# Four attention layers over a 4096-node graph on one core: first products before x, second layer's outputs through PSUM, third layer's rows through DRAM, last masks loaded earlier

## The chip, the core and the metric

The kernel runs on one core of a Trainium2 chip. TensorE (PE) multiplies, VectorE (DVE), ScalarE (ACT) and GpSimd (POOL) work on tiles in on-chip memory (SBUF, and PSUM, into which PE writes), and SyncE (SP) starts most of the transfers from DRAM. Each engine works through its own list of instructions in order and waits for others by semaphores. The metric is the device time of one execution in microseconds (us), lower is better: 2969.83 before, the median of three runs from 2969.72 to 2972.38.

## What is computed

`x` is 4096x256, `adj` a symmetric 4096x4096 matrix of 0 and 1 with ones on the diagonal. Each of four layers attends over the graph's neighbours, adds its input and normalises each row:

```python
def gat(h, adj, W, a):                     # layer 1: 4 heads
    Wh = (h @ W).reshape(n, heads, d)
    e = leaky_relu(s_i[:, None, :] + s_j[None, :, :], 0.2)   # s_i, s_j: Wh times the halves of a
    alpha = softmax(where(adj == 0, -inf, e), axis=1)
    return elu(einsum('ijh,jhd->ihd', alpha, Wh))
def multi_head(x, edge, Wq, bq, Wk, bk, Wv, bv):             # layer 2: 4 heads of 64
    scores = einsum('hnd,hmd->hnm', q, k) / sqrt(64) + (edge.T - 1) * 10000
    return softmax(scores) @ v
# layer 3: as layer 1 with one head of 256 and slope 0.01
def cosine(f, adj, Wq, Wk):                # layer 4
    att = softmax(where(adj > 0, norm(f @ Wk.T) @ norm(f @ Wq.T).T, -9e15))
    return 0.5 * att @ f + 0.5 * f
for layer in (gat, multi_head, gat_one, cosine):
    x = layernorm(x + layer(x))
```

All products are in fp32.

## The kernel before

The rows of the state lie in the SBUF tile `X`, 32 tiles of 128 rows, with one more column of a constant that gives the sums of weights in the last layer. Each layer works on eight blocks `b` of 512 query nodes (`QW`), and in each block on units `j`: 32 tiles of 128 key nodes, in the second layer 64 tiles of 64. A unit builds the unnormalised weights of its keys for the block's queries (`weights`) and then multiplies them with the keys' values into sums in PSUM (`sums`), some units later. At the end of a block its sums are taken out of PSUM, and dividing, adding and normalising them (`outputs`, `finish`) happen in steps between the units of the next block. The outputs of a layer's last block are made in a `tail`, which the next layer calls at a place of its choice.

**First layer** (`additive_heads`, 0 to 727 us). Nodes have two exponentials, `src` and `dst`; a weight is formed from `row`, the `src` values of the block's queries laid along a row and repeated over all partitions (L248), and multiplied with the mask on DVE (L249). For `b` >= 1 the rows go through DRAM (`rows`, L229). For the first block `first_rows` makes them with transposes of broadcast columns (L226), copied out of PSUM at L227. The start runs: L317, one product that spreads the row of `a` over the partitions; `attach` (L101), which multiplies it into the weights on DVE; `turn(0)`, eight transposes of `X` (L111) and their copies to `xT` (L112); `prepare(0)`, eight products of 128x128 by 264 columns (L169, in four groups of key tiles, contraction halves `c` inside); `first_rows`. PE's order is fixed by hand here and in the second layer, elsewhere a scheduler puts the engines' work in order from the program. `narrow` (L816) makes POOL copy one column of a finished weight tile (`tick`) and lets a transfer follow it: the second layer's masks, narrowed to bytes in DRAM.

**Second layer** (`multi_head_attention`; its loop from 822 to 1748 us). A unit is eight matmuls for the scores (L561), the exponential in PSUM on ACT (L563), the mask product on DVE (L566, from PSUM to `prob` in SBUF) and, three units later, eight matmuls for the sums (L587). The sums of the weights, `den`, are gathered beside this: every even unit by POOL (L573, an addition of two SBUF tiles), every odd one by a transfer that accumulates (L579, which POOL issues). The score tiles `p` rotate through three PSUM buffers of two banks each. `finish` takes one of these buffers for the block before, through `halves()`: at j=12 for the sums of `den` (L603), at j=14 for their transposes and reciprocals (L611, L613), at j=17 and 19 for the transposes of half of the block's outputs (L619) each, which DVE multiplies with the reciprocals into the SBUF tile `oh` (L622) and adds to `X` (L627). The roots of the normalising begin at j=29 and end at j=33 (`end_root`, L129 to L132). DVE's and ACT's order is fixed by hand as well.

**Third layer** (`additive_one`, to 2276 us). `prepare(b)` makes `xT`, the values and the rows of one block, four row transposes at L382 among them. Two blocks are prepared first, then comes the second layer's `tail` (L603, L611, L619 and the normalising) and the start of the fourth layer (`follow.start`: its pools and two weight loads on SP), then the loop; during the first block's units the other six blocks are prepared. A unit is four matmuls of 257 columns (L400). A mask transfer on SP covers four units, 1 MB. The sums lie in four banks of the pool `pa` for even blocks and in the four banks `g` of `ps` for odd ones. In the last block, `follow.prepare` makes the fourth layer's inputs for six blocks, at every fifth unit, in the banks of `pa`.

**Fourth layer** (`cosine_attention`). `Cosine.prepare` makes `xT`, queries and keys (L719), their norms (`inverse_root`: L129 to L132) and their transposes `T` (L734). A unit is a product for the scores (L758), an exponential on ACT (L761), the mask on DVE (L762) and, two units later, four matmuls into the sums (L769). A mask transfer, issued by POOL, covers eight units. The third layer's `tail` (the last block's `add_elu` and normalising, small operations of DVE and ACT) and the preparation of the last two blocks come after the second and the thirteenth unit of the first block.

Of the kernel before, what the change touches and what calls it, by code (L numbers as in the profile page):

```python
# [9 lines left out]
FP = mybir.dt.float32  # L10
# [18 lines left out]
def kernel(  # L29
# [53 lines left out]
    def load_x(b, n=QB):  # L83
        for k in range(b * QB, (b + 1) * QB, n):
            nc.sync.dma_start(X[:, k:k + n, :D], xv[:, k:k + n, :])

    def load_w(sb, w, eng):
        eng.dma_start(sb, w.rearrange("(c p) f -> p c f", p=P))
# [73 lines left out]
    def additive_values(xT, b, groups, w_sb, V, src, dst, H, slope):  # L162

        g = 1.0 - slope
        heads = "p k (h d) -> p k h d"
        for k, n, pw in groups:
            for i in range(n):
                for c in range(KC):
                    nc.tensor.matmul(pw[:, i, :D + 2 * H], xT[:, c, (k + i) * P:(k + i + 1) * P], w_sb[:, c, :],  # L169
                                     start=(c == 0), stop=(c == KC - 1))  # L170
# [18 lines left out]
    def additive_heads(a, H, slope, early, narrow, ahead):  # L189
# [7 lines left out]
        with ExitStack() as lay:  # L197
# [23 lines left out]
            def first_rows():  # L221
                row[0] = rp.tile([P, H, QW], FP, name="row")
                for h in range(H):
                    pr = side[:, h, :] if h < HC + 1 else bank()
                    for k in range(QB):
                        nc.tensor.transpose(pr[:, k * P:(k + 1) * P], src[:, k, h:h + 1].to_broadcast([P, P]), ident)  # L226
                    (nc.scalar.copy if h % 2 else nc.vector.tensor_copy)(row[0][:, h, :], pr)  # L227
# [86 lines left out]
            with tc.manual_schedule(engines={mybir.EngineType.PE}):  # L314

                side = pa.tile([P, HC + 1, QW], FP, name="acc")
                nc.tensor.matmul(side[:, 0, :], ones[:1, :], a_row, start=True, stop=True)  # L317
                attach(keep, w_sb, side[:, 0, :], H)
# [4 lines left out]
                for i in range(len(units) + LAG):  # L323
                    if i < len(units):
                        b, j = units[i]
                        weights(b, j)
                        if (b, j) == (1, 4 * QB):
                            early()
                        if i % 8 == 4:
                            narrow(prob[b, j])  # L330
                    if i >= LAG:
# [22 lines left out]
    def additive_one(w_sb, slope, tail, op, follow):  # L354

        MJ = 4
        mvs, taken = {}, {}
        with ExitStack() as lay:
# [6 lines left out]
            sb = pool(lay, "gb_sb", 2)  # L365
            mp = pool(lay, "gb_mask", 3)

            pa = pool(lay, "gb_pa", 1, space=PSUM)
            ps = pool(lay, "gb_ps", 4, space=PSUM)
            edges = adjT.rearrange("(t p) i -> p t i", p=P)  # L370
# [5 lines left out]
            def prepare(b):  # L376
                xT = transposed_block(sb, bank, b)
                groups = [(k, 1, bank().rearrange("p (n f) -> p n f", n=1)) for k in range(QB)]
                additive_values(xT, b, groups, w_sb, V, src, dst, 1, slope)
                pr = bank()  # L380
                for k in range(QB):
                    nc.tensor.transpose(pr[:, k * P:(k + 1) * P], src[:, b * QB + k, :].to_broadcast([P, P]), ident)  # L382
                nc.scalar.copy(row[:, b * QW:(b + 1) * QW], pr)

# [37 lines left out]
            prepare(1)  # L422
            tail(bank)
            follow.start()
            turn = itertools.count()
            units = [(b, j) for b in range(NB) for j in range(NT)]
            for i in range(len(units) + 1):
                if i < len(units):
                    b, j = units[i]
                    weights(b, j)  # L430
                    if b == 0 and j % QB == 2 and j // QB + 2 < NB:
                        prepare(j // QB + 2)
                if i:
                    b, j = units[i - 1]
                    sums(b, j)
                    if b and j % 4 == 0 and j // 4 < QB:
                        outputs(b - 1, j // 4)

                    if b == NB - 1 and j % 5 == 3:
                        follow.prepare(even_bank, j // 5)  # L440
                    if j == NT - 1:
                        take_all(b)
# [7 lines left out]
    def multi_head_attention(w_sb, b_sb, tail, rows_of_den, narrow_edges):  # L450
# [12 lines left out]
        with ExitStack() as lay:  # L463
# [142 lines left out]

            def reciprocals(bank, b):
                s = kept[b]
                pd = bank()
                for k in range(QB):  # L610
                    nc.tensor.transpose(pd[:, k * P:(k + 1) * P], s[:, KC, k * P:(k + 1) * P], ident)  # L611
                rden[b] = fin.tile([P, QB, H], FP, name="rden4")
                nc.vector.reciprocal(rden[b].rearrange("p k h -> p (k h)"), pd[:, ::G])  # L613

            def half(bank, b, k):
                po = bank().rearrange("p (k f) -> p k f", f=D)
                for i in range(2):
                    for c in range(KC):
                        nc.tensor.transpose(po[:, i, c * P:(c + 1) * P],  # L619
                                            kept[b][:, c, (k + i) * P:(k + i + 1) * P], ident)  # L620
                o = fin1.tile([P, 2, D], FP, name="oh")
                nc.vector.tensor_tensor(o.rearrange("p k (h d) -> p (k h) d", h=H),  # L622
                                        po.rearrange("p k (h d) -> p (k h) d", h=H),
                                        rden[b][:, k:k + 2, :].rearrange("p k h -> p (k h)").unsqueeze(2)
                                        .to_broadcast([P, 2 * H, d]), OP.mult)
                y = X[:, b * QB + k:b * QB + k + 2, :D]
                nc.vector.tensor_tensor(y, y, o, OP.add)  # L627

# [6 lines left out]
            def finish(b, j):  # L635
# [4 lines left out]
                elif j == 12:  # L640
                    row_sums(halves(), b)
                elif j == 14:
                    reciprocals(halves(), b)
                elif j in (17, 19):
                    half(halves(), b, j - 17)
                elif j in (21, 23, 25, 27):
# [32 lines left out]
        def tail(bank):  # L679
# [3 lines left out]
            row_sums(bank, b)  # L683
            reciprocals(bank, b)
            half(bank, b, 0)
            half(bank, b, 2)
            mv = fin.tile([P, QB, 2], FP, name="mv")
# [6 lines left out]
    class Cosine:  # L694


        def __init__(self, stack):
            self.stack = stack

        def start(self):  # L700
            keep = self.stack.enter_context(tc.tile_pool(name="co_keep", bufs=1, side="right", reuse_waits="tile"))
            self.pool = self.stack.enter_context(tc.tile_pool(name="co_in", bufs=2, side="right", reuse_waits="tile"))
            self.T = keep.tile([P, 2, N], FP, name="T")
            self.w_sb = keep.tile([P, KC, 2 * P], FP, name="w3_sb")
            load_w(self.w_sb[:, :, :P], wq3T, nc.sync)
            load_w(self.w_sb[:, :, P:], wk3T, nc.sync)

        def prepare(self, bank, b):
# [28 lines left out]
    def cosine_attention(co, tail):  # L737
        MJ = 8
        T, in_ = co.T, co.pool
        with ExitStack() as lay:  # L740
# [3 lines left out]
            pa = pool(lay, "co_pa", 1, space=PSUM)  # L744
            edges = adjT.rearrange("(t p) i -> p t i", p=P)
            ov = out.rearrange("(t p) d -> p t d", p=P)
            mask, acc, prob, y = {}, {}, {}, {}

# [3 lines left out]
            def weights(b, j):  # L752
                cols = slice(b * QW, (b + 1) * QW)
                if j % MJ == 0:
                    mask[b, j // MJ] = sb.tile([P, MJ, QW], BF, name="mask")
                    nc.gpsimd.dma_start(mask[b, j // MJ], edges[:, j:j + MJ, cols])  # L756
                p = bank() if b and j % 2 else pz.tile([P, QW], FP, name="p")
# [3 lines left out]
                nc.scalar.activation(z, p, AF.Exp)  # L761
                nc.vector.tensor_tensor(z, z, mask[b, j // MJ][:, j % MJ, :], OP.mult)  # L762

# [49 lines left out]

    tick = const.tile([P, 1], FP, name="tick")

    def narrow(z):  # L816

        seen = nc.gpsimd.tensor_copy(tick, z[:, 0, :1])  # L818
        for b, j in itertools.islice(todo, 1):
            slim_edges[b, j] = slim.tile([P // 2, NJ, QW], U8, name=f"edges{b}_{j}")  # L820
            with tc.issue_after(getattr(seen, "ins", seen)):
                nc.gpsimd.dma_start(slim_edges[b, j],
# [78 lines left out]
```

## Time and profile before

| | |
|---|---|
| median of the runs | 2969.83 us (2969.72 to 2972.38, three runs) |
| the profiled execution | 2971.39 us |
| its span in the trace | 2969.5 us |
| loops of the layers in the trace | first to 727, second 822 to 1748, third 1748 to 2276, fourth from 2276 |
| a unit of the second layer's loop on PE | 16 matmuls, L561 591 ns and L587 589 ns each by the records, which overlap |
| POOL in the second layer | 248 additions of 2528 ns (L573), 240 transfers issued at 962 ns (L579) |
| mask transfers, third layer | 64 of 1 MB, issued by SP |
| mask transfers, fourth layer | 32 of 1 MB, issued by POOL, 8.4 us from issue to landing |
| first layer's narrowed masks | 32 issues by POOL, 9.4 us to landing, each after a `tick` of 1091 ns |
| data moved | 373.30 MB, 126 GB/s over the span |

The trace names an instruction by line, engine, operation and tiles (`X<-X,oh` writes X and reads X and oh). `x8` merges neighbouring instructions of one kind. In square brackets stands an idle time of the engine before the instruction and what ended it. The granted clock is the share of full speed at which PE was allowed to run.

### The profile page before, as it was taken

Reading aid. Unit: us, or ns where it says so; the run is one execution under the profiler, and the core shown is the slowest. Engines: PE = TensorE matmul, PEld = TensorE weight load, DVE = VectorE, ACT = ScalarE, POOL = GpSimd, SP = SyncE. Lnnn points to the kernel's source line nnn. Section 1 sums busy time; section 2 is a strip of 40 time slices with the busy share of each in tenths; the row PEclk is TensorE's granted clock in tenths of the full one; section 3 lists DMA queues with packets and bytes.
Section 4 is the critical chain, followed back from the end, with each engine's and each line's share of the span. In section 5 each row is a group of like instructions: output and inputs, shape, how many; then the busy total and the mean of one; then the engine's idle time right before and its main releaser. Section 6 shows DMA issues by size and latency. Waiting matters only on the chain.

```text
span 2969.5 us, 50734 instructions
## 1 busy us (share of the span) xinstructions
PE 2925.9 (99%) x20605; PEld 1567.0 (53%) x20605; DVE 1961.3 (66%) x2488; ACT 1672.6 (56%) x2612; POOL 895.7 (30%) x600
## 2 busy tenths in 40 slices
PE   9999999999999999999999999999999999999998
PEld 4333333333633333333333358888887777777776
DVE  7899999997467877877878864655655233333333
ACT  7899999996356656666556554444444222222222
POOL 0000100010078888888889850000000000000000
PEclk9999999999999999999999999999999999999999
DMA  7566566653078888888889773444443232333321
GB/s 198 104 136 140 136 143 136 143 124 73 1 165 190 179 175 189 178 177 192 174 179 189 171 169 100 156 147 151 156 128 57 43 64 50 64 57 58 64 50 22
DMA packets 204956, 373.30 MB, mean 126 GB/s; under 512 B 13249, under 2 KB 89009, under 8 KB 203826
## 3 DMA queue, kind: packets, MB, share of 16 engines
q0 software_dynamic: 101120, 176.18, 36.8%
q1 hardware_dynamic: 103328, 193.62, 19.6%
q8 instruction: 161, 2.64, 0.4%
q14 instruction: 73, 0.60, 0.1%
q10 hardware_dynamic: 274, 0.26, 0.0%
HBM read 315.43 MB, written 21.03 MB: 113 GB/s over the span
## 4 chain that ended last, share of the span: by engine, by line
PE 95%; DVE 2%; ACT 1%; DMA 1%; issue 0%; POOL 0%; DVEq 0%; POOLq 0%; ACTq 0%
PE acc L259 22%; PE acc L769 15%; PE p L561 14%; PE acc L587 13%; PE acc L400 8%; PE g L400 7%; PE p L758 4%; PE g L758 3%; PE g L489 2%; DVE prob L566 1%; PE g L503 1%; PE g L169 1%; ACT p L563 1%; PE acc L169 1%; PE acc L719 1%; PE g L111 1%
## 5 line engine op out<-in xcount | busy, mean ns | idle before, releaser
L566 DVE TENSOR_TENSOR prob<-p,mask 128x1024 f32<-128x1024 f32 x512 | 620.4, 1222 | 201.8 <-ACT p L563 197.5
L563 ACT ACTIVATE p<-p,shift 128x1024 f32<-128x1024 f32 x512 | 555.6, 1088 | 350.1 <-PE p L561 341.4
L259 PE MATMUL acc<-prob,V 128*32 128x512 f32 x6144 | 663.8, 592 | 0.0
L573 POOL TENSOR_TENSOR den<-den,prob 128x1024 f32<-128x1024 f32 x248 | 626.9, 2528 | 65.7 <-DVE prob L566 55.2
L248 ACT ACTIVATE prob<-row,dst 128x512 f32<-128x512 f32 x1024 | 635.6, 710 | 1.7 <-DVE row L227 1.7
L249 DVE SCALAR_TENSOR_TENSOR prob<-prob,mask 128x2048 f32<-128x2048 f32 x256 | 582.6, 2287 | 24.5 <-ACT prob L248 21.5
L561 PE MATMUL p<-qT,kT 64*64 64x512 f32 x4096 | 532.1, 591 | 15.2 <-DVE prob L566 14.4
L587 PE MATMUL acc<-prob,V 64*64 64x512 f32 x4096 | 530.2, 589 | 3.9 <-DVE kept L592 3.9
L769 PE MATMUL acc<-X,prob 128*128 128x257 f32 x2048 | 486.8, 381 | 4.3 <-DVE prob L762 4.3
L769 PEld LDWEIGHTS acc<-X,prob 128*128 128x128 f32 x2048 | 389.0, 190 | 166.8 <-issue 114.8
L762 DVE TENSOR_TENSOR prob<-prob,mask 128x512 f32<-128x512 f32 x256 | 176.8, 691 | 423.8 <-ACT prob L761 418.5
L259 PEld LDWEIGHTS acc<-prob,V 128*32 128x32 f32 x6144 | 197.4, 110 | 451.6 <-issue 433.2
L756 POOL DMA_DIRECT2D mask<-in_adjT x32 | 28.1, 879 | 1106.1 <-DVE prob L762 561.1
L392 ACT ACTIVATE e<-row,dst 128x512 f32<-128x512 f32 x256 | 184.1, 721 | 239.1 <-DVE prob L394 209.5
L561 PEld LDWEIGHTS p<-qT,kT 64*64 64x64 f32 x4096 | 152.3, 133 | 296.6 <-issue 247.2
L587 PEld LDWEIGHTS acc<-prob,V 64*64 64x64 f32 x4096 | 155.8, 133 | 289.3 <-issue 278.2
L394 DVE SCALAR_TENSOR_TENSOR prob<-e,mask 128x512 f32<-128x512 f32 x256 | 176.3, 689 | 179.6 <-PE acc L400 97.4
L579 POOL DMA_DIRECT2D den<-prob x240 | 231.0, 962 | 52.8 <-DVE prob L566 47.9
L761 ACT ACTIVATE prob<-p 128x512 f32<-128x512 f32 x144 | 85.9, 597 | 259.3 <-PE p L758 245.3
L818 POOL COPY tick<-prob 128x1 f32<-128x1 f32 x32 | 34.9, 1091 | 651.6 <-DVE prob L249 651.6
L400 PE MATMUL g<-V,prob 128*128 128x257 f32 x1024 | 226.5, 380 | 0.0
L400 PE MATMUL acc<-V,prob 128*128 128x257 f32 x1024 | 225.8, 381 | 0.0
(147 smaller groups left out, 1992.4 us busy)
## 6 DMA issues: line engine op xcount, KB each, us to landing
den<-prob POOLq DMA_DIRECT2D x240, 512.0 KB, 5.2
mask<-in_adjT SPq DMA_DIRECT2D x128, 512.0 KB
mask<-in_adjT SPq DMA_DIRECT2D x64, 1024.0 KB
mask<-edges SPq DMA_DIRECT2D x256, 128.0 KB
mask<-in_adjT POOLq DMA_DIRECT2D x32, 1024.0 KB, 8.4
edges<-in_adj POOLq DMA_DIRECT2D x32, 512.0 KB, 9.4
den<-prob SPq DMA_DIRECT2D x16, 512.0 KB
row<-far SPq DMA_DIRECT2D x7, 1024.0 KB
```

The source lines that it names most:

```text
L248: nc.scalar.activation(z[:, h, :], row[b][:, h, :], AF.Relu, bias=-1.0, scale=dst[:, j, h:h + 1])
L249: nc.vector.scalar_tensor_tensor(z, z, 1.0, mask[m][:, j % MJ, :].unsqueeze(1).to_broadcast([P, H, QW]), OP.add, OP.mult)
L259: nc.tensor.matmul(acc[b][h * G:(h + 1) * G, n, :], part, prob[b, j][:, h, :], start=(j == 0), stop=(j == NT - 1))
L400: nc.tensor.matmul(acc[b][k][:, :D + 1], prob[b, j][:, k * P:(k + 1) * P], V[:, j, :], start=(j == 0), stop=(j == NT - 1))
L561: nc.tensor.matmul(p[c * d:(c + 1) * d, r, :], kT[half, c, j * d:(j + 1) * d], qT[half, c, cols], start=True, stop=True)
L563: nc.scalar.activation(p, p, AF.Exp, bias=shift)
L566: nc.vector.tensor_tensor(z, p, mask[m][:, j % MJ, :].unsqueeze(1).to_broadcast([P, KC, QW]), OP.mult)
L573: nc.gpsimd.tensor_tensor(to, to, flat, OP.add)
L579: nc.gpsimd.dma_start(to, flat, accum_op=OP.add)
L587: nc.tensor.matmul(acc[b][r * d:(r + 1) * d, c, :], V[half, j, r * d:(r + 1) * d], prob[b, j][half, r, :], start=(j == 0), stop=(j == NH - 1))
L758: nc.tensor.matmul(p, T[:, 0, j * P:(j + 1) * P], T[:, 1, cols], start=True, stop=True)
L769: nc.tensor.matmul(acc[b][k], prob[b, j][:, k * P:(k + 1) * P], X[:, j, :], start=(j == 0), stop=(j == NT - 1))
```

## The change

Seven things change; the values computed are the same.

1. Start: five products of `ones` with `ones` go into a part of `side` that L317 does not write, ahead of L317. `additive_values` goes through the contraction halves outside and through the group's key tiles inside. `first_rows` takes the banks `bank()` for odd heads and `side` for even ones.
2. `tick` moves up and gets a helper `behind(z)`; `narrow` uses it.
3. Second layer: `reciprocals` and `half` lose their transposes to `turned_row_sums` and `turned_half`. The product with the reciprocals is written in place in PSUM, and the addition reads it there. The steps j=14, 17 and 19 become two, j=15 and 18.
4. Third layer: masks of two units in four buffers in place of four units in three. For `b` >= 1 the row goes by SP to a DRAM tile and is read back broadcast. The pools `ps` and `pa` are opened in the other order.
5. The second layer's tail and the fourth layer's start come after the third unit's sums of the first block.
6. The fourth layer's masks: transfers of four units in a pool of their own with four buffers. Three of them are issued in the last block of the third layer, each behind a tick on a weight tile.
7. `follow.prepare` runs at every fourth unit, the first at j=2.

```diff
+    tick = const.tile([P, 1], FP, name="tick")
+    def behind(z):
+        seen = nc.gpsimd.tensor_copy(tick, z)
+        return tc.issue_after(getattr(seen, "ins", seen))
...
@@ additive_values
-            for i in range(n):
-                for c in range(KC):
+            for c in range(KC):
+                for i in range(n):
...
@@ first_rows
-                    pr = side[:, h, :] if h < HC + 1 else bank()
+                    pr = bank() if h % 2 else side[:, h, :]
...
@@ additive_heads, start
                 side = pa.tile([P, HC + 1, QW], FP, name="acc")
+                for _ in range(5):
+                    nc.tensor.matmul(side[:, 1, :P], ones, ones, start=True, stop=True)
                 nc.tensor.matmul(side[:, 0, :], ones[:1, :], a_row, start=True, stop=True)
...
-                            narrow(prob[b, j])
+                            narrow(prob[b, j][:, 0, :1])
...
@@ additive_one
-        MJ = 4
+        MJ = 2
...
-            mp = pool(lay, "gb_mask", 3)
+            mp = pool(lay, "gb_mask", 4)
+            dr = pool(lay, "gb_dram", 2, space=bass.MemoryType.DRAM)
+            ps = pool(lay, "gb_ps", 4, space=PSUM)
             pa = pool(lay, "gb_pa", 1, space=PSUM)
-            ps = pool(lay, "gb_ps", 4, space=PSUM)
...
+                part = row[:, b * QW:(b + 1) * QW]
+                if b:
+                    far = dr.tile([QB, P], FP, name="far")
+                    nc.sync.dma_start(far.rearrange("k p -> p k"), src[:, b * QB:(b + 1) * QB, 0])
+                    nc.sync.dma_start(part, far.rearrange("k p -> (k p)").unsqueeze(0).to_broadcast([P, QW]))
+                    return
                 pr = bank()
...
-                nc.scalar.copy(row[:, b * QW:(b + 1) * QW], pr)
+                nc.scalar.copy(part, pr)
...
             prepare(0)
             prepare(1)
-            tail(bank)
-            follow.start()
...
                     sums(b, j)
+                    if (b, j) == (0, 2):
+                        tail(bank)
+                        follow.start()
...
-                    if b == NB - 1 and j % 5 == 3:
-                        follow.prepare(even_bank, j // 5)
+                    if b == NB - 1 and j in (6, 10, 14):
+                        follow.load_mask(0, (j - 6) // 4, prob[b, j][:, :1])
+                    if b == NB - 1 and j % 4 == 2 and j // 4 < NB - 2:
+                        follow.prepare(even_bank, j // 4)
...
@@ multi_head_attention
-            def reciprocals(bank, b):
-                s = kept[b]
+            def turned_row_sums(bank, b):
                 pd = bank()
                 for k in range(QB):
-                    nc.tensor.transpose(pd[:, k * P:(k + 1) * P], s[:, KC, k * P:(k + 1) * P], ident)
+                    nc.tensor.transpose(pd[:, k * P:(k + 1) * P], kept[b][:, KC, k * P:(k + 1) * P], ident)
+                return pd
...
+            def half(po, b, k):
+                heads = po.rearrange("p k (h d) -> p (k h) d", h=H)
+                nc.vector.tensor_tensor(heads, heads, rden[b][:, k:k + 2, :].rearrange("p k h -> p (k h)").unsqueeze(2)
                                         .to_broadcast([P, 2 * H, d]), OP.mult)
                 y = X[:, b * QB + k:b * QB + k + 2, :D]
-                nc.vector.tensor_tensor(y, y, o, OP.add)
+                nc.vector.tensor_tensor(y, po, y, OP.add)
...
-                elif j == 14:
-                    reciprocals(halves(), b)
-                elif j in (17, 19):
-                    half(halves(), b, j - 17)
+                elif j == 15:
+                    bank = halves()
+                    pd = turned_row_sums(bank, b)
+                    po = turned_half(bank, b, 0)
+                    reciprocals(pd, b)
+                    half(po, b, 0)
+                elif j == 18:
+                    half(turned_half(halves(), b, 2), b, 2)
...
@@ Cosine
+        MJ = 4
...
+            self.masks = self.stack.enter_context(tc.tile_pool(name="co_mask", bufs=4, side="right", reuse_waits="tile"))
+            self.mask = {}
...
+        def load_mask(self, b, m, seen=None):
+            mask = self.mask[b, m] = self.masks.tile([P, self.MJ, QW], BF, name="mask")
+            part = adjT.rearrange("(t p) i -> p t i", p=P)[:, m * self.MJ:(m + 1) * self.MJ, b * QW:(b + 1) * QW]
+            with behind(seen) if seen is not None else nullcontext():
+                nc.gpsimd.dma_start(mask, part)
...
@@ cosine_attention, weights
-                if j % MJ == 0:
-                    mask[b, j // MJ] = sb.tile([P, MJ, QW], BF, name="mask")
-                    nc.gpsimd.dma_start(mask[b, j // MJ], edges[:, j:j + MJ, cols])
+                m = b, j // MJ
+                if m not in co.mask:
+                    co.load_mask(*m)
...
-                nc.vector.tensor_tensor(z, z, mask[b, j // MJ][:, j % MJ, :], OP.mult)
+                nc.vector.tensor_tensor(z, z, co.mask[m][:, j % MJ, :], OP.mult)
```

More of the change, by code (lines that the diff above doesn't have):

```diff
@@ L1 @@
 import itertools
-from contextlib import ExitStack
+from contextlib import ExitStack, nullcontext
 import concourse.bass as bass
@@ L605, in row_sums, with turned_half @@
                 nc.scalar.copy(kept[b][:, KC, :], pd)
-            def reciprocals(bank, b):
-                s = kept[b]
+            def turned_row_sums(bank, b):
                 pd = bank()
                 for k in range(QB):
-                    nc.tensor.transpose(pd[:, k * P:(k + 1) * P], s[:, KC, k * P:(k + 1) * P], ident)
-                rden[b] = fin.tile([P, QB, H], FP, name="rden4")
-                nc.vector.reciprocal(rden[b].rearrange("p k h -> p (k h)"), pd[:, ::G])
-            def half(bank, b, k):
+                    nc.tensor.transpose(pd[:, k * P:(k + 1) * P], kept[b][:, KC, k * P:(k + 1) * P], ident)
+                return pd
+            def turned_half(bank, b, k):
                 po = bank().rearrange("p (k f) -> p k f", f=D)
@@ L620, in half, with reciprocals @@
                                             kept[b][:, c, (k + i) * P:(k + i + 1) * P], ident)
[L621 to L624, printed above, removed]
+                return po
+            def reciprocals(pd, b):
+                rden[b] = fin.tile([P, QB, H], FP, name="rden4")
+                nc.vector.reciprocal(rden[b].rearrange("p k h -> p (k h)"), pd[:, ::G])
+            def half(po, b, k):
+                heads = po.rearrange("p k (h d) -> p (k h) d", h=H)
+                nc.vector.tensor_tensor(heads, heads, rden[b][:, k:k + 2, :].rearrange("p k h -> p (k h)").unsqueeze(2)
                                         .to_broadcast([P, 2 * H, d]), OP.mult)
                 y = X[:, b * QB + k:b * QB + k + 2, :D]
-                nc.vector.tensor_tensor(y, y, o, OP.add)
+                nc.vector.tensor_tensor(y, po, y, OP.add)
             def halves():
@@ L683, in tail @@
             row_sums(bank, b)
-            reciprocals(bank, b)
-            half(bank, b, 0)
-            half(bank, b, 2)
+            reciprocals(turned_row_sums(bank, b), b)
+            for k in (0, 2):
+                half(turned_half(bank, b, k), b, k)
             mv = fin.tile([P, QB, 2], FP, name="mv")
@@ L737, in cosine_attention @@
     def cosine_attention(co, tail):
-        MJ = 8
+        MJ = co.MJ
         T, in_ = co.T, co.pool
@@ L744, in cosine_attention @@
             pa = pool(lay, "co_pa", 1, space=PSUM)
-            edges = adjT.rearrange("(t p) i -> p t i", p=P)
             ov = out.rearrange("(t p) d -> p t d", p=P)
-            mask, acc, prob, y = {}, {}, {}, {}
+            acc, prob, y = {}, {}, {}
             def bank():
@@ L812 @@
     todo = iter([(b, j) for b in range(NB) for j in range(0, 2 * NT, NJ)])
-    tick = const.tile([P, 1], FP, name="tick")
     def narrow(z):
-        seen = nc.gpsimd.tensor_copy(tick, z[:, 0, :1])
         for b, j in itertools.islice(todo, 1):
             slim_edges[b, j] = slim.tile([P // 2, NJ, QW], U8, name=f"edges{b}_{j}")
-            with tc.issue_after(getattr(seen, "ins", seen)):
+            with behind(z):
                 nc.gpsimd.dma_start(slim_edges[b, j],
```

## The prediction

> **What bounds the kernel now.** I read the page's totals first, then the sums by stage, then the waits of TensorE (PE), then the timeline at each place where PE waits.
>
> ```profile
> PE 2925.9 (99%) x20605; PEld 1567.0 (53%) x20605; DVE 1961.3 (66%) x2488; ACT 1672.6 (56%) x2612; POOL 895.7 (30%) x600
> ```
>
> PE is busy 2925.9 of 2969.5 us, so only two things can move the time: the 43.6 us in which PE idles, and work or slow clock inside its busy time. The sums by stage (columns: stretch, its length, then the busy time of PE, PEld, DVE, ACT and POOL, the granted clock, DMA) say where the idle time lies:
>
> ```profile
> 0.00:822.00 822.00, 814.85 (x7169) 302.33 (x7173) 710.96 (x653) 693.49 (x1202) 58.88 (x70) 1.00 0.55 120
> 822.00:1747.90 925.90, 907.54 (x8332) 317.77 (x8324) 721.45 (x687) 565.47 (x540) 803.24 (x495) 1.00 0.86 181
> 1747.90:1853.30 105.40, 101.51 (x505) 84.67 (x502) 49.27 (x102) 44.53 (x152) 5.49 (x3) 0.98 0.38 118
> 2186.30:2287.20 100.90, 94.43 (x463) 76.09 (x461) 57.04 (x139) 49.94 (x167) 2.75 (x3) 1.00 0.26 68
> ```
>
> Second layer 18.4 us idle, first layer 7.2, the hand-over to the third 3.9, to the fourth 6.5. All four are places the change touches. Two of PE's waits (us, times, longest):
>
> ```profile
> PE p L561 <- DVE prob L566: 14.4, 15, 1.5
> PE g L603 <- POOL den L595: 2.6, 1, 2.6
> ```
>
> **Second layer, outputs through PSUM.** Here the tile view, the timeline of the third block and PE's wait belong together:
>
> ```profile
> L627 DVE TENSOR_TENSOR X<-X,oh x16: 677/2434/3028, 971.1 to 1770.5; 128x512 f32<-128x512 f32 x16
> L622 DVE TENSOR_TENSOR oh<-p,rden x14: 675/678/681, 970.4 to 1674.3; 128x512 f32<-128x512 f32 x14
> ...
> 1087.36 2.36 POOL L573 TENSOR_TENSOR den<-den,prob 128x1024 f32<-128x1024 f32 x1 [0.65 <-DVE prob L566]
> ...
> 1091.46 1.09 PE L561 MATMUL p<-qT,kT 64*64 64x512 f32 x8 [1.50 <-DVE prob L566]
> ```
>
> L627 adds two SBUF tiles. It takes 2.43 us in the 14 cases where POOL's L573 runs beside it, and 0.69 in the two of the tail, where POOL is idle. L622, the same size with one operand in PSUM, takes 0.68 beside the same L573. The changed add reads the product from PSUM, so I price it by L622: 14 x (2.43 - 0.69) = 24 us less DVE. What reaches PE is less: in seven blocks PE stands before L561 after the second half, 1.2 to 1.6 us beyond a normal step (8.9 in all by the starts of L619 and L561), and loses another 0.13 two units later (0.9). The merged step at j=15 also makes one interruption of the product stream fewer, 0.11 + 0.09 us by its neighbours' steps, x7 = 1.4. Sum 11.2; taken 11. Does the longer hold of the PSUM buffer make a new wait? From rows: exp starts 1.11 after L561, DVE 1.12 after that, 1.22 long, so a buffer is free 3.5 us after its product. At j=15 reciprocal 0.25, product 0.68 and add 0.69 follow the mask product and free the buffer 5.1 us after the step's L561 began; PE wants it at 6.2. At j=18, 4.9 against 5.8. So no. The in-place product into PSUM has no row on DVE; nearest is L622 (0.68) below, L627's 2.43 above. Ends: 3 (a wait remains) to 16 (the 0.85 us waits at the root, L131, six times, vanish too).
>
> **Start.** Columns: start, duration.
>
> ```profile
> 2.24 2.04 PE L317 MATMUL acc<-a_row,ones 1*128 1x512 f32 x2 [2.24 <-DMA a_row<-in_a]
> 4.21 2.24 PE L111 MATMUL g<-ident,X 128*128 128x128 f32 x8
> 7.45 5.62 PE L169 MATMUL acc<-w_sb,xT 128*128 128x264 f32 x12 [1.00 <-ACT xT L112]
> 21.20 2.84 PE L169 MATMUL acc<-w_sb,xT 128*128 128x264 f32 x12
> ```
>
> The same twelve passes cost 5.62 at first and 2.84 later: passes step at 440 ns until 12.4 us, at 222 after. Five products of ones are ten passes of 128 columns, at the cold step of 213 ns (L111) 2.1 us: from the end of the memset (1.01) to 3.3. L317 then runs at about 3.3 to 5.1; its reader, the DVE product L101, waited until 5.21 for w_sb anyway, so nothing is lost. The transposes end about 6.8 instead of 6.45, L169 begins 6.85 instead of 7.45, since the turned loop needs only the first half of xT and w_sb for six passes. PE is then busy without a break from 1.1. Ends: -0.3 (clock as before, all 0.3 later) to 0.6 + 2.78 = 3.4. The granted clock reads 1.00 in the first 14 us although the passes step at half rate, but it shows the slow state after the two later idles (this is the first of them):
>
> ```profile
> 1764.00:1766.00 2.00, 2.00 (x6) 1.52 (x7) 0.00 (x0) 0.58 (x1) 0.00 (x0) 0.50 0.26 72
> 1766.00:1768.00 2.00, 2.00 (x13) 2.00 (x12) 0.67 (x2) 0.00 (x0) 0.00 (x0) 0.65 0.23 67
> ```
>
> Work resumed at 1762.9 and 2287.2; steps were full again at 1767.4 and 2292.9, and at the start 5.0 us after 7.45: 4.5 to 5.7 unbroken us each. From 1.1 that is 5.6 to 6.8, before L169. I take 2.9, near the upper end.
>
> [...]
>
> First rows: PE waits 0.8 + 0.7 for copies out of the tile that all heads share; two heads now go elsewhere, but the transposes after them still wait for the last copy on ACT: 0.9 net (0.5 to 1.4). PE runs ahead into work whose inputs were ready (L259 shows no wait), so the sum, 3.8, stays.
>
> **Hand-over to the third layer.**
>
> ```profile
> 1762.88 1.06 PE L603 MATMUL g<-den,ones 64*32 64x512 f32 x8 [2.57 <-POOL den L595]
> 1763.87 2.01 PE L400 MATMUL acc<-V,prob 128*128 128x257 f32 x4
> ```
>
> PE stands for POOL, 2.8 us from start to start, then runs cold (four passes at 430 ns or more instead of 217, eight transposes at 213 instead of 109: 1.8). In the changed order three units (twelve products) and the preparation of block 2 stand ahead of L603, which PE reaches near 1769, after POOL's 1762.8. Also gone: 0.85 before L111 for the kept copy, since preparation moves to the banks that the products leave first. 5.4, less 0.8 for the copy of xT still waited for: 4.6. Seven blocks lose four row transposes, 0.59 each from L382's start (1776.17) to the next product (1776.76): 4.1. Together 8.7 (5 to 9.5).
>
> Hidden work: the rows go SP to DRAM and back. The store of 4-byte pieces has no row; nearest are bq_sb (1.04 us of SP) below and POOL's 9.4 us landing above. Block 1's row is wanted 32 units, 55 us, later. Behind the row load, which waits on SP for the store, stand the masks: 512 KB each, four buffers, eight units (13.9 us) deep; a 1 MB mask issued at 1842.0 had moved by 1846.4. 64 more mask issues of 0.4 us are 26 us of an idle SP queue. The two weight loads of the fourth layer move behind seven masks and are wanted 400 us later. [...]
>
> **Hand-over to the fourth layer.**
>
> ```profile
> 2278.39 1.06 PE L734 MATMUL acc<-ident,rows 128*128 128x128 f32 x8 [1.92 <-DVE rows L730]
> 2286.45 0.69 DVE L762 TENSOR_TENSOR prob<-prob,mask 128x512 f32<-128x512 f32 x1 [4.18 <-DMA mask<-in_adjT]
> 2287.20 2.08 PE L769 MATMUL acc<-X,prob 128*128 128x257 f32 x4 [4.29 <-DVE prob L762]
> 2289.08 4.72 PE L719 MATMUL g<-w_sb,xT 128*128 128x256 f32 x12
> ```
>
> The last L400 ends at 2276.48 (E). Mask and last preparation now come early. What is late next is DVE: sixteen small operations of the third layer's end stand before L762; from their times before (2275.21 to 2281.74, less 1.8 for the row chain between) L762 ends at E+4.15 and L769 starts at E+4.25 (10.72 before). L719 then waits for DVE's xT, E+6.4, runs warm in 2.6 and PE is at the next L769 at E+9.1, where it was at E+17.15: 8.0 (3.5 if DVE is slower by half, 9.6 if its waits close). The first p of the fourth layer now takes a bank of the last block's sums, free at E-0.4: no wait. POOL's three ticks (1.09) and 32 more issues (0.88) meet an idle POOL; a tick holds one of three prob buffers for 1 us of 5. Preparations every 4 units instead of 5 in the block with the old outputs: 1 us lost.
>
> **Sum.** 3.8 + 11 + 8.7 + 8 - 1 = 30.5. The profiled execution took 2971.4 (span 2969.5 and 1.9 around it); less 30.5 that is 2940.9. The median of the runs is 1.6 lower: 2939.3, said as 2939.
>
> **Rivals.** (a) The PSUM form does not free DVE from POOL: no row has DVE writing PSUM in place. The 11 fall to 1: 2949. L566 and L622, undisturbed beside L573, speak against it. (b) DVE holds the fourth layer's start and the clock stays cold at the beginning: 4 and 2 lost: 2945. (c) Slower: masks of the third layer come late, because four buffers of two units leave 10.4 us (13.9 less the 3.5 of use) where three of four left more. From a landing over 10.4 us each of 32 rounds loses the excess; 36 us, and so slower by 0.2%, from 11.6; at 12, 51 us, 2990. POOL's 9.4 us landings are the row for it, the 4.4 us above against. (d) Waits only move: as much reappears on DVE or ACT in each stage, 2966; against it, DVE is busy 66% and ACT 56%.
>
> **Chances.** Forecast 0.62, (a) 0.13, (b) 0.12, (c) 0.06, (d) 0.07 (its 2966 is within what can be told). What a measurement can tell from no change is 0.2%, 6 us. Faster 0.88, same 0.06, slower 0.06. The range goes from all upper ends together (4.8 + 16 + 9.5 + 9.6 - 1 = 39: 2931, 2930 with the reading's spread) past (a) and (b) to 2953, where (a) and half of (b) meet.
>
> **What would show it.** L627's successor at 0.7 us, no wait over 0.3 after the halves; L169's first twelve passes under 4 us; L603 without wait; the fourth layer's first L769 4 to 5 us after the last third-layer product. Wrong if mask waits appear in the third layer, or the add still takes 2.4 us.

## The result and the profile after

The changed kernel takes 2961.5 us (median of six runs, 2959.78 to 2961.84) against 2970.4 in as many runs of the kernel before: ratio 0.9967, 95% interval 0.9954 to 0.998. It is faster by 9 us, where 30.5 were forecast. Its profiled span is 2959.8 us, 9.7 less than before.

The page's totals and the sums by stage of the changed kernel (columns as before: stretch, length, busy time of PE, PEld, DVE, ACT, POOL, granted clock, DMA):

```profile
PE 2920.2 (99%) x20587; PEld 1567.0 (53%) x20587; DVE 1940.8 (66%) x2488; ACT 1666.7 (56%) x2605; POOL 920.6 (31%) x635
```

```profile
0.00:820.58 820.58, 815.99 (x7179) 304.30 (x7183) 711.02 (x653) 693.38 (x1202) 65.21 (x70) 1.00 0.58 121
820.58:1734.12 913.54, 903.78 (x8332) 319.33 (x8324) 701.29 (x687) 565.58 (x540) 801.79 (x495) 1.00 0.87 184
1734.12:1847.20 113.08, 97.90 (x477) 81.53 (x473) 48.24 (x97) 38.44 (x144) 5.51 (x3) 0.96 0.50 111
2182.50:2279.50 97.00, 95.28 (x463) 76.16 (x462) 56.10 (x137) 48.97 (x165) 3.63 (x7) 1.00 0.37 87
```

The second layer's loop is 12.4 us shorter and DVE's busy time there 20 us less. The stretch from its end to the third layer's second block, 105.4 before, is 113.1: PE is idle 15.2 us of it, and the granted clock has a mean of 0.96. Cut at the starts of PE's products, from the first layer's last product to the second's last sums, from there to the last third-layer product, and on to the end, the spans differ from before by -1.4 (first layer), -12.4, +12.1 and -8.1: together -9.7. The third layer, which should have gained, lost.

The waits that are new, PE's, DVE's and SP's (total, times, longest):

```profile
PE g L417 <- DVE prob L411: 7.9, 1, 7.9
PE acc L417 <- DVE prob L411: 4.9, 2, 2.5
```

```profile
DVE prob L411 <- DMA mask<-in_adjT: 28.9, 5, 11.6
```

```profile
SPq L395 <- DMA far<-src: 75.7, 7, 12.3
```

PE waits for weights (L417 for L411), they wait for masks, and SP, which issues the masks, stands 75.7 us at the load of the row (L395) until the store (L394) has landed. SP's timeline shows it for one block, and below it stand two stretches by the sums (the first within this wait):

```profile
1782.03 0.34 SPq L395 DMA_DIRECT2D row<-far  x1
1782.46 0.39 SPq L407 DMA_DIRECT2D mask<-in_adjT  x1
1782.94 0.42 SPq L394 DMA_DIRECT2D far<-src  x1
1794.50 0.34 SPq L395 DMA_DIRECT2D row<-far  x1
1794.93 0.90 SPq L407 DMA_DIRECT2D mask<-in_adjT  x2
1795.88 1.80 SPq L394 DMA_DIRECT2D far<-src  x1
```

```profile
1787.50:1794.40 6.90, 6.90 (x33) 6.05 (x32) 3.23 (x7) 2.37 (x12) 0.00 (x0) 1.00 0.00 0
1820.00:1824.00 4.00, 1.70 (x8) 1.14 (x6) 0.59 (x1) 0.00 (x0) 0.00 (x0) 1.00 0.00 0
```

For 6.9 us nothing moves at all (DMA share 0.00, 0 GB/s): the store's small packets have gone by (560 packets under 512 bytes from 1782.9 to 1787.5, the store's 512 among them), SP goes on to the load only at 1794.50, and the masks are not issued. In the second stretch PE works 1.7 of 4 us, also with nothing moving.

### The profile page after: what moved, and what is told of

Same layout as the page of the kernel before. It is cut to its first block, busy times and chain, and to the rows that moved or that the text cites. A ratio compares the mean times of both kernels' runs of the same rounds, so it can differ in the third digit from the quotient of the medians.

```text
span 2959.8 us, 50964 instructions
## 1 busy us (share of the span) xinstructions
PE 2920.2 (99%) x20587; PEld 1567.0 (53%) x20587; DVE 1940.8 (66%) x2488; ACT 1666.7 (56%) x2605; POOL 920.6 (31%) x635
## 4 chain that ended last, share of the span: by engine, by line
PE 94%; DVE 3%; DMA 2%; ACT 1%; issue 0%; SPq 0%; DVEq 0%; ACTq 0%
PE acc L266 22%; PE acc L806 15%; PE p L581 14%; PE acc L607 14%; PE g L417 7%; PE acc L417 7%; PE p L795 4%; PE g L795 3%; PE g L509 2%; PE g L523 1%; PE g L176 1%; DMA far<-src 1%; PE acc L176 1%; DVE prob L586 1%; PE acc L757 1%; DMA mask<-in_adjT 1%
## 5 line engine op out<-in xcount | busy, mean ns | idle before, releaser
L593 POOL TENSOR_TENSOR den<-den,prob 128x1024 f32<-128x1024 f32 x248 | 613.7, 2475 | 76.9 <-DVE prob L586 63.7
L806 PE MATMUL acc<-X,prob 128*128 128x257 f32 x2048 | 485.7, 380 | 0.0
L806 PEld LDWEIGHTS acc<-X,prob 128*128 128x128 f32 x2048 | 388.5, 190 | 162.1 <-issue 114.1
L91 POOL COPY tick<-prob 128x1 f32<-128x1 f32 x35 | 41.8, 1193 | 1114.2 <-DVE prob L256 643.8
L411 DVE SCALAR_TENSOR_TENSOR prob<-e,mask 128x512 f32<-128x512 f32 x256 | 176.7, 692 | 192.8 <-PE acc L417 82.5
L744 POOL DMA_DIRECT2D mask<-in_adjT x64 | 47.5, 743 | 641.8 <-DVE prob L799 490.8
L417 PE MATMUL g<-V,prob 128*128 128x257 f32 x1024 | 229.0, 382 | 7.9 <-DVE prob L411 7.9
L417 PE MATMUL acc<-V,prob 128*128 128x257 f32 x1024 | 227.3, 382 | 4.9 <-DVE prob L411 4.9
L599 POOL DMA_DIRECT2D den<-prob x240 | 221.3, 922 | 31.0 <-DVE prob L586 25.3
```

The lines of the kernel that those rows point to most:

```text
L417: nc.tensor.matmul(acc[b][k][:, :D + 1], prob[b, j][:, k * P:(k + 1) * P], V[:, j, :], start=(j == 0), stop=(j == NT - 1))
L593: nc.gpsimd.tensor_tensor(to, to, flat, OP.add)
L599: nc.gpsimd.dma_start(to, flat, accum_op=OP.add)
L806: nc.tensor.matmul(acc[b][k], prob[b, j][:, k * P:(k + 1) * P], X[:, j, :], start=(j == 0), stop=(j == NT - 1))
```

## Experiments

**The row's path.** Four kernels, each the changed one with another way for the third layer's row. The first moves one line, and the lists of PE, DVE and ACT stay as they are:

```diff
-                    nc.sync.dma_start(part, far.rearrange(...))
+                    nc.gpsimd.dma_start(part, far.rearrange(...))
```

> The changed kernel with one line different: the load of the row (L395) is issued by POOL instead of SP; the store of 4-byte pieces (L394) stays on SP ahead of the masks, and the lists of PE, DVE and ACT are the same. Theory: what costs is that SP stands at L395 for the store's landing (11 to 13 us each from L394's issue to L395's, seven times) with the third layer's masks behind it; PE then loses 12.8 us in three waits for L411 and about 5 more in half-speed passes after them. If so the waits go and the time falls by 16 to 19, from 2961.5 to 2943 to 2946. Rival: the 512 small pieces themselves hold the transfers of the masks behind them in the same queue; then masks stay late and the time stays above 2955. Second rival: four buffers of two units are too few for the masks whatever SP does; also above 2955.

Measured: 2944.06 (ratio to before 0.9908, interval 0.9894 to 0.9921). The second moves the store too:

> Store and load of the rows both issued by POOL. Theory (SP's wait is the cause): as with the load alone on POOL, 2943 to 2946, within 1 us of it. Rival (the small pieces hold SP's queue): this one is fast, 2943 to 2946, and the one with the store left on SP is not. Second rival (too few mask buffers): above 2955 here too.

Measured: 2945.25 (0.9911, 0.9898 to 0.9925). The third makes all rows with PE's four transposes, by leaving out the branch `if b:`.

> The rows are made by four transposes on PE for every block, as before the change; all else of the changed kernel stays, masks of two units in four buffers too. Theory: no mask waits; the stalls' 16 to 19 are gained and the 0.59 x 7 = 4.1 us of transposes come back: 2947 to 2950. Rival (too few mask buffers): mask waits stay and the time is above 2957.

Measured: 2948.12 (0.992, 0.9907 to 0.9934). The fourth keeps the way over SP and changes the size of the pieces:

```diff
-                    nc.sync.dma_start(far.rearrange("k p -> p k"), src[:, b * QB:(b + 1) * QB, 0])
+                    nc.tensor.transpose(pr[:QB, :P], src[:, b * QB:(b + 1) * QB, 0], ident)
+                    nc.scalar.copy(line, pr[:QB, :P])
+                    nc.sync.dma_start(far, line)
```

> The row goes through DRAM by SP still, but one transpose turns the 128x4 block first and ACT copies it, so that the store moves four pieces of 512 bytes instead of 512 of 4. In the first layer such stores let SP go on 1.1 us after the last of them. Theory: the store's landing depends on the size of the pieces; SP stands for about 2 us instead of 12, no mask waits, and PE pays one transpose of about 0.2 us per block: 2944 to 2948. Rival (any pass through DRAM of a store that is waited for costs SP its 12 us, whatever the pieces): still 2958 or more.

Measured: 2943.49 (0.9907, 0.9893 to 0.9921). All four gain what the theory said. Two numbers miss narrowly: the two kernels with POOL lie 1.2 us apart where 1 was said, within the scatter of their runs, and the fourth is 0.5 faster than its range. With the load on POOL the wait is still there, only nothing stands behind it; with pieces of 512 bytes SP waits 0.9 us at most. POOL's waits of the first kernel, then SP's timeline of the fourth:

```profile
POOL row L395 <- DMA far<-src: 73.8, 7, 16.1
```

```profile
1779.88 0.27 SPq L398 DMA_DIRECT2D far<-line  x1
1781.06 0.34 SPq L399 DMA_DIRECT2D row<-far  x1
1782.49 3.92 SPq L411 DMA_DIRECT2D mask<-in_adjT  x2
1791.47 0.27 SPq L398 DMA_DIRECT2D far<-line  x1
```

From store to load 1.18 us, where the same 2 KB in pieces of 4 bytes took 11.56 above. (Size and number of the pieces change together here, so the two are not told apart.) Neither traffic nor buffers were at fault: the store stays in SP's queue ahead of the masks in the first kernel, and four buffers of two units stay in all four, without a wait for a mask that PE notices. The rows' transposes cost 2948.12 - 2944.06 = 4.1 us, the 0.59 x 7 of the prediction.

**Second layer: the kernel before with its halves' outputs in PSUM alone** (the product in place, the addition reads it, steps as they were):

```diff
-                o = fin1.tile([P, 2, D], FP, name="oh")
-                nc.vector.tensor_tensor(o..., po..., rden...)
+                nc.vector.tensor_tensor(heads, heads, rden...)
...
-                nc.vector.tensor_tensor(y, y, o, OP.add)
+                nc.vector.tensor_tensor(y, po, y, OP.add)
```

> The kernel before with one part of the change: the product with the reciprocals stays in PSUM and the addition reads it there; the steps stay at j=14, 17 and 19. Theory: the addition falls from 2.43 us to about 0.69 in 14 cases, and the second layer's part of the span (1021.1 from the first layer's last product to the last sums) shortens by the waits after the second half, 8.9 to 10.9 us, of the 12.4 that the whole change shortened it by; 2959.5 to 2962. Rival: the place of the operands does nothing and the merged steps j=15 and 18 made the difference: 2969 to 2971.

Measured: 2961.78 (0.9962, 0.9949 to 0.9974); the second layer's part of the span is 1011.0, 10.1 less than before. In the changed kernel, which also merges the steps, it is 1008.8, 2.2 less again. The addition in the changed kernel, by its line:

```profile
L651 DVE TENSOR_TENSOR X<-p,X x14: 691/692/694, 965.9 to 1660.0; 128x512 f32<-128x512 f32 x14
```

**Start.** The kernel with the row's load on POOL, without the products of ones, and with 20 of them (`range(5)` left out, or `range(20)`).

> As the kernel with the row's load on POOL (2944.06), without the five products of ones. In the five profiles with them the clock rises 11.2 to 12.7 us after the start, between passes of L176, and the first sums L266 begin at 23.1 to 24.3; without them (the kernel before) it rose at 12.95. Theory now: the products of ones warm nothing, because the clock rises only after a stretch that begins with L176; they even hold L327 back by 1.25 us and attach's chain by 0.4. Then the clock rises between 10.9 and 14.3, L176 starts at 7.4 instead of 7.8, and the time is 2943 to 2945. Rival (the prediction's reading: the run of work since 1.06 counts): L176 runs cold 3 us longer than with them, 2946 to 2947.

> As the kernel with the row's load on POOL, with 20 products of ones instead of five: over 4 us of nothing but full products from 1.06 us. A probe of the clock; it holds up L327 and what follows. If products of ones count, the passes step at half the duration from some point between 4.5 and 8 us, still within the products of ones, and L176 starts warm near 12. If they do not count, they run cold to about 9.6, L176 starts cold near 14, and the clock rises behind it, at 17 to 21.

Measured: 2944.49 without them, within the runs of 2944.06 with them: no difference can be told. The clock rose at 13.5 (there the passes' step falls from 440 to 223 ns), inside the theory's stretch; L176 started at 7.92, not at 7.4. With 20 it rose at 7.15, among the products of ones: they do count, and the theory that they do not is wrong. This one run took 2946.79. Starts and durations on PE, first five products (the changed kernel), then twenty:

```profile
1.06 2.50 PE L326 MATMUL acc<-ones 128*128 128x128 f32 x10 [1.06 <-DVE X L80]
3.49 2.07 PE L327 MATMUL acc<-a_row,ones 1*128 1x512 f32 x2
5.49 1.97 PE L118 MATMUL g<-ident,X 128*128 128x128 f32 x8
7.83 4.88 PE L176 MATMUL acc<-w_sb,xT 128*128 128x264 f32 x12 [0.37 <-issue]
```

```profile
1.06 7.62 PE L326 MATMUL acc<-ones 128*128 128x128 f32 x40 [1.06 <-DVE X L80]
9.66 1.09 PE L118 MATMUL g<-ident,X 128*128 128x128 f32 x8
12.00 2.91 PE L176 MATMUL acc<-w_sb,xT 128*128 128x264 f32 x12 [1.25 <-ACT xT L119]
```

Five are 2.5 us of work, then follow a product of one row and transposes, and L176 still starts cold (4.88 where 2.84 is warm). In nine profiles with five products the clock rose between 9.7 and 12.7, in three without them between 10.8 and 13.5. Twenty warm the clock, but L327 then comes 5 us later and L176 starts 4 us later. What the one-row product and the transposes count for was not separated.

**Hand-overs.** Two parts undone in the kernel with the row's load on POOL: the tail and the fourth layer's start back ahead of the loop, and the first three masks issued only behind `take_all` of the last block.

> As the kernel with the row's load on POOL (2944.06), with the second layer's tail and the fourth layer's start ahead of the third layer's loop again. Theory: L623 then stands ahead of the first units and waits for POOL again, 2.8 us, and PE runs cold after it, 1.8; with the wait for the kept copy 0.85 at most: 3.5 to 5.5 slower, 2947.5 to 2949.5. Rival: the other order of the PSUM pools and the rows without transposes took the wait away: 2944 to 2945.

> As the kernel with the row's load on POOL (2944.06), with the first three masks of the fourth layer issued by POOL behind the first sum that is taken out of PSUM at the third layer's end, where the fourth layer still needs 4.4 us to its first L799. A tick (1.2), the issue (0.7) and 5.7 us to landing put that L799 3 to 4 us later. Theory: PE waits that much more and then runs cold for up to 5 us: 3 to 6 us slower, 2947 to 2950. Rival: DVE's work for the last block sets the start anyway: 2944 to 2945.

Measured: 2948.17 (0.9922, 0.9905 to 0.9938), 4.1 slower than with the tail in the loop; PE waits again, here 3.8 us, and from 1749.5 the granted clock is 0.5 for 3.4 us:

```profile
PE g L622 <- POOL den L614: 3.8, 1, 3.8
```

Late masks: 2946.68 (0.9914, 0.9899 to 0.9929), 2.6 slower, just under what was expected; by the trace the fourth layer reaches its second block 3.4 us later.

**The root.** The largest stall left in the second layer, about 0.85 us in each of seven blocks, stands behind the multiply-add L138. Both kernels change it in the kernel with pieces of 512 bytes.

```diff
-        nc.vector.tensor_scalar(s, s, -0.5, 1.5, OP.mult, OP.add)
+        nc.vector.tensor_scalar(s, s, newton[:, 0:1], newton[:, 1:2], OP.mult, OP.add)
```

> As the kernel with rows in pieces of 512 bytes (2943.49), with one more edit: the multiply-add of the root (L138), 128x4 in SBUF, takes its two constants from columns of a tile instead of immediate numbers, as L154 does. In the changed kernel L138 takes 2.5 us when POOL's L593 runs (6 of 7), and PE then stands 0.85 us; L154, 128x256 with scalars from a tile, took 0.41 beside L593 in 8 cases. Theory: the form with immediate numbers is what L593 holds up; the root falls to 0.2 us and PE's seven waits go: 5 to 6.5 us, 2937 to 2938.5. Rival: any DVE operation from SBUF to SBUF that starts just behind L593 is held: 2943 to 2944.

Measured: 2942.83 (0.9899, 0.9885 to 0.9912) and the operation as slow as ever: a miss. The eight cases of L154 "beside L593" that spoke for it had started in the addition's last 0.05 to 0.3 us, and so showed nothing. (The next expectation misreads one row: the two products start 0.24 and 0.05 us ahead of POOL's addition, not 0.35 and 0.15.) Next, only the place was changed:

```diff
                 elif j == 33:
-                    end_root(*roots[b])
-                elif j in (35, 37, 39, 41):
+                    middle[b] = middle_root(*roots[b])
+                elif j == 35:
+                    end_root(*roots[b], middle[b])
+                elif j in (37, 39, 41, 43):
```

> As the kernel with rows in pieces of 512 bytes (2943.49), with the root's end cut in two: its first two products stay at j=33, the multiply-add and the last product come at j=35, and the four scalings at j=37 to 43. With the constants from a tile the multiply-add still took 2.49 us in 7 of 7, each time starting 0.14 us after L593, while the two products before it started 0.35 and 0.15 us ahead of L593 and took 0.16. Theory: what decides is the start, ahead of POOL's addition or behind it; two operations fit ahead of it, four do not. Then the seven waits of PE go, 0.85 each, the second layer's part falls from 1008.7 to about 1003, and the time is 2937 to 2938.5. Rival: PE's wait at the root has another cause (the number of small DVE operations): 2942 to 2944.

Measured: 2937.45 (2937.30 to 2937.93; 0.9885, 0.9869 to 0.9902), the fastest here. DVE's timeline at a root with constants from a tile and POOL's beside it, then the same two for the root in two steps:

```profile
1111.48 0.15 DVE L139 TENSOR_TENSOR s<-r 128x4 f32<-128x4 f32 x1
1111.66 0.16 DVE L140 TENSOR_TENSOR s<-s,v 128x4 f32<-128x4 f32 x1
1111.86 2.50 DVE L141 TENSOR_SCALAR s<-s,newton 128x4 f32<-128x4 f32 x1
```

```profile
1111.72 2.61 POOL L600 TENSOR_TENSOR den<-den,prob 128x1024 f32<-128x1024 f32 x1
```

```profile
1110.27 0.15 DVE L136 TENSOR_TENSOR s<-r 128x4 f32<-128x4 f32 x1
1110.46 0.16 DVE L137 TENSOR_TENSOR s<-s,v 128x4 f32<-128x4 f32 x1
...
1113.72 0.16 DVE L144 TENSOR_SCALAR s<-s 128x4 f32<-128x4 f32 x1
```

```profile
1110.52 2.64 POOL L603 TENSOR_TENSOR den<-den,prob 128x1024 f32<-128x1024 f32 x1
1112.83 1.15 POOL L609 DMA_DIRECT2D den<-prob  x1
```

The first two start ahead of POOL's addition. The multiply-add, one step later, falls where POOL issues a transfer and takes 0.16 us, in its old form. The layer's part shortens from 1008.7 to 1002.9. The run shows that the multiply-add is fast (0.16 us) where no addition of POOL runs; that a start ahead of the addition is enough, as the theory says, it does not show (see the last section).

## Why the prediction was wrong

The direction held; the time lay 8.5 us outside the range. The step that put it there is "Hidden work" in the hand-over to the third layer: "Behind the row load, which waits on SP for the store, stand the masks", priced at nothing. The runs put 17.4 us on it; without that wait on SP the time is 2944.06, inside the range. A second term, the start, was sized too large by 2.4. The terms, in us of the profiled spans (the last column is the run with the row's load on POOL):

| term | forecast gain | changed kernel | row's load on POOL |
|---|---|---|---|
| start | 3.8 | 1.4 | 0.9 |
| second layer | 11 | 12.4 | 12.4 |
| hand-over to the third, its first block | 8.7 | -7.8 | 7.6 |
| its second block | 0 | -2.3 | 0 |
| last block, hand-over to the fourth | 8 - 1 | 6.0 | 5.7 |
| sum | 30.5 | 9.7 | 26.6 |

*Hidden work of the rows.* The wait was seen, and set once against eight units of cover, 13.9 us. The sum over a round was not made. PE needs a preparation and four units, two masks, every 11.47 us (the distance of the preparations in the kernel with the load on POOL). SP needs the store, its landing, the load and two masks: 11.7, 12.9, 15.5 and 14.0 us from one store to the next in the last four rounds. From the first of the seven stores to the last SP takes 80.2 us, and 68.7 in the kernel with the load on POOL. A queue that needs longer for a round than its reader uses up its cover if enough rounds stand in a row, and here there are seven. It also took the wrong nearest rows, a load of 1.04 us and a landing of 9.4, and mentioned the waiting only with regard to the block that wants the row. In the first layer a store and load of the same kind, in 512-byte pieces, let SP go on 0.9 to 1.1 us after the last store's issue had ended (seven blocks of the changed kernel, L243 and L245); that row was the one to ask why the new store should differ. The loss in this step is 2961.5 - 2944.06 = 17.4 us by the runs; by the spans 15.4 in the first block and 2.3 in the second, and of these 12.8 in PE's three waits and most of the rest in passes at half rate after them (granted clock 0.50 from 1824.3 to 1827.7 and from 1841.4 to 1851.6).

The rival (c) had the right symptom, late masks, but another mechanism: it made them late by buffers and by a landing over 10.4 us in all 32 rounds. The runs show one block with late masks, from SP's queue, and none with the same four buffers once SP was free. Rival (a) fell with the outputs in PSUM alone; of (b) the cold start came true and DVE's hold on the fourth layer did not.

What set the new store apart from the first layer's is how it is divided: in 512 pieces of 4 bytes SP's load starts 11.56 us after the store, in four of 512 bytes, the same 2 KB, 1.18. Why the store of small pieces lands late no run shows.

*Start.* 1.4 for 3.8, by mis-sizing the clock term: the work from 1.06 us was taken for one unbroken run that ends the cold stretch by 6.8. The transposes ended at 7.46 and L176 began at 7.83, where 6.8 and 6.85 were forecast, and the clock rose at 11.8, among L176's products, as in the kernel before. The bound of -0.3 had been named; the value was taken near the wrong end. In the nine profiles with five products the first layer's last product starts between 723.8 and 725.7 us, so 1.4 and 0.9 are the same within this spread. What the turned loop and the first rows gained was not measured apart.

*Second layer.* Right in mechanism and size: the addition at 0.69 us, no wait after the halves, 10.1 from the operands in PSUM and 2.2 from merging, where 1.4 was said. The root's waits stayed, as the value of 11 assumed.

*Hand-overs.* To the third layer 7.6 for 8.7 once SP is free: 4.1 for the transposes (forecast 4.1), 4.1 by runs or 3.7 by spans for the tail's place (forecast 4.6). To the fourth, the first L806 starts at 2279.55, 4.7 us after the last L417 ends (forecast 4.25), and 6.0 of 7 were gained; the early masks hold 2.6 of it.

## What to carry to other kernels

When a step is moved to a queue, add up the queue's whole round, waits for landings included, and set it against the round of whoever it feeds; cover only helps against what happens once (here SP took 80.2 us from the first store to the last, against 68.7 with the load on POOL). A load that reads back a store belongs in a queue with nothing urgent behind it (here POOL's: 2944.06 against 2961.5), and a store of 4-byte pieces is worth turning on chip first (here into pieces of 512 bytes: 1.18 us from store to load against 11.56, and 2943.49). And a short operation that is slow now and then should be looked up by what runs beside it when it starts, before its form is changed (here 2.5 us behind POOL's addition in both forms, 0.16 one step later in the old one).

## What the runs showed that was not expected

A multiply-add of 128x4 on DVE that starts 0.14 us behind POOL's addition ends 0.04 us after it, with immediate constants (2.52 us, six of seven) and with constants from a tile (2.49, seven of seven). The products that start 0.05 us or more ahead of the addition take 0.16, and the mask products that read PSUM beside it their 1.22. But the seventh multiply-add of the changed kernel started 0.12 us ahead by the records, and was held all the same:

```profile
1341.94 2.81 DVE L138 TENSOR_SCALAR s<-s 128x4 f32<-128x4 f32 x1
```

```profile
1342.06 2.65 POOL L593 TENSOR_TENSOR den<-den,prob 128x1024 f32<-128x1024 f32 x1
```

In the kernel before two more did the same (2.79 and 2.87 us, 0.10 and 0.17 ahead). So the recorded start alone does not decide; whether a multiply-add and a product differ here was not tested.

The granted clock of the changed kernel is 0.50 for 3.41 us from 1824.3, 1.00 for the next 13.65 and 0.50 for 10.24 after that, 1, 4 and 3 times 3.41; in the kernel before, the first two stretches at 0.50 are 3.41 and 6.83 us long. In the nine starts with five products the rise lay up to 3.0 us apart. Whether the one has to do with the other was not shown: between 5.5 and 14 us, where the passes' step changes, the granted clock reads 1.00.
